# A norm applied on the transposed side: 1/std as a row through HBM, the mean folded into the weights

## The chip, the cores and the metric

The kernel runs on one core of a Trainium2 chip. The time is the device time in microseconds of that core, from the first to the last instruction. Engines are named as in the profile: PE (TensorE matmuls), PEld (its weight loads), DVE (VectorE), ACT (ScalarE), POOL (GpSimd), SP (SyncE, which here only issues transfers).

## The reference, cut to what matters

The input is (4, 128, 128, 128) in fp32: four images of 128 channels and 128 x 128 pixels. Layer 0 is a block that works on each pixel (token) by itself; layer 1 is a 3 x 3 convolution with a squeeze gate.

```python
def _block(x, ...):                       # every token t has 128 channels c
    t = x.reshape(b, c, h * w).transpose(0, 2, 1)
    t = _ln(t, ln0_g, ln0_b)
    y1 = _ln(t, ln1_g, ln1_b)
    att = jnp.einsum('btc,oc->bto', jax.nn.sigmoid(y1) * y1, W_out)
    t = t + att
    y2 = _ln(t, ln2_g, ln2_b)             # the norm that the change is about
    wht = jnp.einsum('btc,oc->bto', y2, W_whiten)
    k = jnp.square(jax.nn.relu(jnp.einsum('btc,hc->bth', wht, W_key)))      # 512 hidden
    kv = jnp.einsum('bth,ch->btc', k, W_value)
    r = jax.nn.sigmoid(jnp.einsum('btc,oc->bto', wht, W_recep))
    t = t + r * kv
    return t.transpose(0, 2, 1).reshape(b, c, h, w)
# _ln: (x - mean) * rsqrt(var + 1e-5) * g + b, over the 128 channels of a token
# ... layer 0: x = x + block(gn(x)) + the same block on the image turned; as the block works
#     on single tokens, both give the same, and the kernel computes it once
# ... layer 1: x = x + conv3x3(gn(x)) * gate
```

## The kernel before

Layer 0 handles a *group* of two chunks (h = 0, 1) of 512 pixels each. A group g passes through the operations of the list ORDER. One pass of the list is a *slot*: in slot s an entry `op:k` is issued for group s - k. Each engine runs its instructions in the order in which they are issued, so the list fixes the order on every engine. There are 64 groups; 20 slots after an image's first group its convolution begins, in the same slots.

```python
ORDER = """
    u1:0 Tu1:0 Tz21:3 u0:0 e1:1 bn01:0 Tu0:0 re02:3 tt0:2 bn00:0 c0:1 cp1:3 sq01:3 c2:1 S0:2
    q2:1 a:1 re00:3 y0:1 Tz11:1 pk10:3 z10:1 silu1:1 pk13:3 nb0:0 Tz10:1 re10:3 c5:1 re13:3
    y3:1 sq00:3 att1:1 pr0:3 p2:1 silu0:1 nb2:2 sq03:3 v0b:1 kv00:3 kv01:3 sq02:3 in1:0 b:1
    t1:0 att0:1 g1:0 v3:1 v4:1 v5a:0 th0:3 kv02:3 t0:0 in0:0 z20:2 b1:0 g0:0 pk12:3 pr1:3
    re12:3 bn11:0 T1:1 c3:1 sq12:3 T0:1 kv03:3 q0:3 pk11:3 e3:1 th1:3 sq13:3 v5b:0 Tz20:2
    b0:0 cp0:2 bn10:0 tt1:2 c4:0 re11:3 bn21:1 sq10:3 c:0 y2:0 kv10:3 x10:3 d:0 sq11:3 y1:0
    z21:2 pk03:2 S1:2 kv11:3 ca:0 q:0 pk01:2 p:0 kv12:3 bx0:3 kv13:3 nb1:0 v1:0 q1:3 x11:3
    bn20:1 c1:0 bx1:3 z11:0 re01:2 re03:2 pk00:2 v2:0 pk02:2 v0a:0 d8:0
"""

SQUARES = ("PAAA", "PAAA")

ON_GPSIMD = set()
ODD = {"v5a", "v5b", "c4", "c", "d", "y1", "y2", "ca", "d8", "c0", "y0", "c5", "y3"}
EVEN = {
    "p", "q", "v1", "v2", "p2", "q2", "c1", "e1", "c2", "a", "b", "v3", "v4", "c3", "e3",
```

The operations with their engines: `u` group norm of the input (ACT), `Tu` its transpose (PE), `bn` statistics per token (DVE), `nb` the terms of a norm (POOL), `t` norm 0 applied (ACT), `g`, `b` gain and shift (POOL), `z1`, `z2` norm 1 and norm 2 applied (ACT), `Tz` transposes of z (PE), `silu` (ACT), `att` (PE), `T` adds it to t (DVE), `cp` the input of the hidden layer brought from PSUM (ACT), `pk`, `pr`, `kv` the large matmuls (PE), `re`, `th` ReLU and tanh (ACT), `sq` the square (ACT or POOL, by SQUARES), `tt` the transpose of t for the residual (PE), `S`, `q` (DVE), `x` (POOL), `bx` and `in` statistics of the images (DVE). The names without a digit pair (`p`, `v1`, `c1`, `y0` and so on) are the convolution: `c` is PE, `e` ACT, the rest DVE.

Norm 0 and norm 1 and norm 2 are all applied with tokens on the partitions, where mean and 1/std of a token are scalars of a partition; the matmuls need channels on the partitions, so each z is transposed afterwards. PSUM banks come by tag; `tr` has two, used in turn.

```python
    def turned(src, tag, name):
        pt = bank(tag, name).rearrange("p (s c) -> p s c", s=SUB)
        for s in range(SUB):
            nc.tensor.transpose(pt[:, s, :], src[:, s, :], ident)
        return pt

    def scaled(dst, src, norm, h):
        rs, nb = norm
        for s in range(SUB):
            i = h * SUB + s
            nc.scalar.activation(
                dst[:, s, :], src[:, s, :], AF.Identity,
                bias=nb[:, i : i + 1], scale=rs[:, i : i + 1],
            )
    # ...
    def norm_terms(k, g):
        # ...
        gp, rs, nb, sm = nc.gpsimd, term("rs"), term("nb"), term("sm")
        gp.tensor_tensor(rs, st[:, :, 1], st[:, :, 4], ALU.subtract)
        gp.tensor_tensor(rs, rs, rs, ALU.mult)
        gp.tensor_scalar(rs, rs, C / 4, C * LN_EPS, ALU.mult, ALU.add)
        gp.tensor_tensor(sm, st[:, :, 2], st[:, :, 5], ALU.add)
        gp.tensor_tensor(rs, rs, sm, ALU.add)
        gp.tensor_tensor(rs, rs, nhalf, ALU.pow)
        gp.tensor_tensor(sm, st[:, :, 1], st[:, :, 4], ALU.add)
        gp.tensor_tensor(sm, sm, nhalf, ALU.mult)
        gp.tensor_tensor(nb, sm, rs, ALU.mult)
        S["norm", k, g] = rs, nb
    # ...
    def norm(k, g, h):
        S[f"z{k}", g, h] = z = sub_tile("z", "z", 3)
        scaled(z, S["t", g][:, h], S["norm", k, g], h)

    def norm_turned(k, g, h):
        S[f"z{k}t", g, h] = turned(S.pop((f"z{k}", g, h)), "tr", f"z{k}t")
    # ...
    def key_input(g, h):
        S["y2", g, h] = y = wk.tile([P, CH], F32, tag="y2", name="y2")
        nc.scalar.copy(y, flat(S.pop(("z2t", g, h))))

    def key(g, h, j):
        S["pk", g, h, j] = pk = bank("h", "pk")
        nc.tensor.matmul(pk, wk_s[:, ts(j, P)], S["y2", g, h], start=True, stop=True)
    # ...
    def t_turned(g, h):
        S["tt", g, h] = turned(S["t", g][:, h], "tr", "tt")

    def add_t(g, h):
        xs = chunk_of(g, h)
        nc.vector.scalar_tensor_tensor(
            xs, flat(S.pop(("tt", g, h))), 2.0, xs, ALU.mult, ALU.add
        )
```

The weights of the hidden layer are made once: the whitening matrix times the key and receptance matrices, with the gain of norm 2.

```python
    for src, n, dst, bias in ((wkt, HID, wk_s, kbias), (wrt, P, wr_s, rbias)):
        pw = bank("h", "pw")
        nc.tensor.matmul(pw[:, :n], ww, src, start=True, stop=True)
        raw = staged("raw", n)
        nc.vector.tensor_copy(raw, pw[:, :n])
        nc.vector.tensor_scalar(dst, raw, g2, None, ALU.mult)
        # ... the biases
```

Of the kernel before, what the change touches and what calls it, by code (L numbers as in the profile page):

```python
# [9 lines left out]
F32 = mybir.dt.float32  # L10
AF = mybir.ActivationFunctionType
ALU = mybir.AluOpType

P = 128
CH = 512
SUB = CH // P
# [6 lines left out]


ORDER = """
    u1:0 Tu1:0 Tz21:3 u0:0 e1:1 bn01:0 Tu0:0 re02:3 tt0:2 bn00:0 c0:1 cp1:3 sq01:3 c2:1 S0:2
    q2:1 a:1 re00:3 y0:1 Tz11:1 pk10:3 z10:1 silu1:1 pk13:3 nb0:0 Tz10:1 re10:3 c5:1 re13:3
    y3:1 sq00:3 att1:1 pr0:3 p2:1 silu0:1 nb2:2 sq03:3 v0b:1 kv00:3 kv01:3 sq02:3 in1:0 b:1
    t1:0 att0:1 g1:0 v3:1 v4:1 v5a:0 th0:3 kv02:3 t0:0 in0:0 z20:2 b1:0 g0:0 pk12:3 pr1:3
    re12:3 bn11:0 T1:1 c3:1 sq12:3 T0:1 kv03:3 q0:3 pk11:3 e3:1 th1:3 sq13:3 v5b:0 Tz20:2  # L30
    b0:0 cp0:2 bn10:0 tt1:2 c4:0 re11:3 bn21:1 sq10:3 c:0 y2:0 kv10:3 x10:3 d:0 sq11:3 y1:0
    z21:2 pk03:2 S1:2 kv11:3 ca:0 q:0 pk01:2 p:0 kv12:3 bx0:3 kv13:3 nb1:0 v1:0 q1:3 x11:3
    bn20:1 c1:0 bx1:3 z11:0 re01:2 re03:2 pk00:2 v2:0 pk02:2 v0a:0 d8:0
"""

SQUARES = ("PAAA", "PAAA")

ON_GPSIMD = set()
ODD = {"v5a", "v5b", "c4", "c", "d", "y1", "y2", "ca", "d8", "c0", "y0", "c5", "y3"}
# [7 lines left out]
def conv_preact_kernel(  # L47
# [40 lines left out]
    nc = tc.nc  # L88
    B, C, H, W = x.shape
    HID = w_key_t.shape[1]  # L90
# [7 lines left out]
    N = PAIR * SUB  # L98
# [3 lines left out]
    const = ctx.enter_context(tc.tile_pool(name="const", bufs=1))  # L102
# [2 lines left out]
    wk = ctx.enter_context(tc.tile_pool(name="wk", bufs=2))  # L105
    small = ctx.enter_context(tc.tile_pool(name="small", bufs=4))
    stat = ctx.enter_context(tc.tile_pool(name="stat", bufs=2))
    ps = ctx.enter_context(tc.tile_pool(name="ps", bufs=2, space=bass.MemoryType.PSUM))

    def bank(tag, name, bufs=2):  # L110
        return ps.tile([P, CH], F32, tag=tag, name=name, bufs=bufs)
# [30 lines left out]

    nhalf = const.tile([P, N], F32, tag="nhalf", name="nhalf")
    nc.gpsimd.memset(nhalf, -0.5)
    ones = const.tile([P, P], F32, tag="ones", name="ones")
    nc.gpsimd.memset(ones, 1.0)

    def load_const(name, src, shape):
        t = const.tile(shape, F32, tag=name, name=name)
# [22 lines left out]

    wk_s = const.tile([P, HID], F32, tag="wk_s", name="wk_s")
    wr_s = const.tile([P, P], F32, tag="wr_s", name="wr_s")
    kbias = const.tile([P, NH], F32, tag="kbias", name="kbias")
# [2 lines left out]
    def staged(name, n):  # L180
        return wk.tile([P, n], F32, tag="h", name=name, bufs=6)
# [5 lines left out]
    for src, n, dst, bias in ((wkt, HID, wk_s, kbias), (wrt, P, wr_s, rbias)):  # L187
        pw = bank("h", "pw")
        nc.tensor.matmul(pw[:, :n], ww, src, start=True, stop=True)
        raw = staged("raw", n)  # L190
        nc.vector.tensor_copy(raw, pw[:, :n])
        nc.vector.tensor_scalar(dst, raw, g2, None, ALU.mult)
        pb = bank("h", "pb")
        for j in range(n // P):
            nc.tensor.matmul(pb[:, j : j + 1], raw[:, ts(j, P)], b2, start=True, stop=True)
        nc.vector.tensor_copy(bias, pb[:, : n // P])
# [37 lines left out]
    def conv_setup(b):  # L234

        cw = wg.tile([P, 9, P], F32, tag="ring", name="cw", bufs=1)
        nc.sync.dma_start(cw, conv_w)
        d, mg, rs = yield from group_norm(st1.pop(b), "1")  # L240
        avg = col("avg")
        nc.vector.tensor_tensor(avg, d, rs, ALU.mult)
        mg6 = col("mg6")
        nc.vector.tensor_scalar(mg6, mg, 6.0, None, ALU.mult)
        yield
        p1 = bank("h", "p1")
        nc.tensor.matmul(p1[:NSE, 0:1], s1, avg, start=True, stop=True)
        yield
        a1 = stat.tile([NSE, 1], F32, tag="a1", name="a1")
        nc.vector.tensor_scalar(a1, p1[:NSE, 0:1], 0.0, None, ALU.max)  # L250
        yield
        p2 = bank("h", "p2")
        nc.tensor.matmul(p2[:, 0:1], s2, a1, start=True, stop=True)
        yield
        se = col("se")
        nc.scalar.activation(se, p2[:, 0:1], AF.Tanh, scale=0.5)
        yield
        nc.vector.tensor_scalar(se, se, 1.0, 0.5, ALU.add, ALU.mult)
        beta = col("beta")
        nc.vector.scalar_tensor_tensor(beta, se, cb, mg, ALU.mult, ALU.add)  # L260
        dg = wk.tile([P, P], F32, tag="u", name="dg")
        nc.vector.tensor_scalar(dg, ident, se, None, ALU.mult)
        yield
        pg = bank("h", "pg")
        nc.tensor.matmul(pg[:, :P], ones, dg, start=True, stop=True)
        yield
        row = wk.tile([P, P], F32, tag="u", name="row")
        nc.scalar.copy(row, pg[:, :P])
        yield
        nc.vector.scalar_tensor_tensor(  # L270
            cw, cw, rs, row.rearrange("p (o c) -> p o c", o=1).to_broadcast([P, 9, P]),
            ALU.mult, ALU.mult,
        )
        nc.vector.tensor_tensor(cw[:, 4], cw[:, 4], ident, ALU.add)
        yield
        w0, w1, w2 = (cw[:, 3 * a : 3 * a + 3].rearrange("p b c -> p (b c)") for a in range(3))
# [12 lines left out]
        yield
        for i in (1, 2):  # L290
            yield from form(i, None)
        nc.vector.scalar_tensor_tensor(u[1], tmp, -1.0 / 6, w6, ALU.mult, ALU.subtract)
        nc.vector.scalar_tensor_tensor(u[2], tmp, -1.0 / 6, w6, ALU.mult, ALU.add)
        yield
        w4 = wk.tile([P, 3 * P], F32, tag="z", name="w4", bufs=3)
        nc.scalar.mul(w4, w0, 0.25)
        nc.scalar.mul(w6, w6, 0.5)
        nc.vector.tensor_tensor(tmp, w4, w2, ALU.add)
        yield
        yield from form(3, None)  # L300
        yield from form(4, 1)
        nc.vector.scalar_tensor_tensor(u[3], tmp, 1.0 / 6, w6, ALU.mult, ALU.add)
        nc.vector.scalar_tensor_tensor(u[4], tmp, 1.0 / 6, w6, ALU.mult, ALU.subtract)
        yield
        yield from form(0, 2)
        nc.scalar.copy(u[0], w4)
        yield
        yield from form(5, 3)
        nc.scalar.copy(u[5], w2)
        gn1[b] = mg, mg6, beta  # L310
        uws[b] = uw

# [28 lines left out]
    def sub_tile(tag, name, bufs):  # L341
        return wk.tile([P, SUB, C], F32, tag=tag, name=name, bufs=bufs)
# [19 lines left out]
    def norm_terms(k, g):  # L362

        st = S.pop(("st", k, g))

        def term(name):
            return small.tile([P, N], F32, tag=f"{name}{k}", name=name, bufs=2)
# [5 lines that stand above are left out]
        gp.tensor_tensor(sm, st[:, :, 2], st[:, :, 5], ALU.add)  # L375
        gp.tensor_tensor(rs, rs, sm, ALU.add)
        gp.tensor_tensor(rs, rs, nhalf, ALU.pow)  # L377
        gp.tensor_tensor(sm, st[:, :, 1], st[:, :, 4], ALU.add)
        gp.tensor_tensor(sm, sm, nhalf, ALU.mult)
        gp.tensor_tensor(nb, sm, rs, ALU.mult)  # L380
        S["norm", k, g] = rs, nb

    def first_norm(g, h):
        if ("t", g) not in S:
# [9 lines left out]
        nc.gpsimd.tensor_tensor(t, t, over(b0), ALU.add)  # L394

    def norm(k, g, h):
        S[f"z{k}", g, h] = z = sub_tile("z", "z", 3)
        scaled(z, S["t", g][:, h], S["norm", k, g], h)

    def norm_turned(k, g, h):  # L400
# [12 lines left out]
    def attended(g, h):  # L413
        t = flat(S["t", g][:, h])
        nc.vector.tensor_tensor(t, S.pop(("att", g, h)), t, ALU.add)

    def key_input(g, h):
        S["y2", g, h] = y = wk.tile([P, CH], F32, tag="y2", name="y2")
        nc.scalar.copy(y, flat(S.pop(("z2t", g, h))))

    def key(g, h, j):
        S["pk", g, h, j] = pk = bank("h", "pk")
# [34 lines left out]
    def add_t(g, h):  # L457
        xs = chunk_of(g, h)
        nc.vector.scalar_tensor_tensor(
            xs, flat(S.pop(("tt", g, h))), 2.0, xs, ALU.mult, ALU.add  # L460
        )

    def gated(g, h):
# [140 lines left out]
    def layer0_op(op, g):  # L604
# [12 lines left out]
            "silu": lambda: silu(g, *d),  # L617
            "att": lambda: attend(g, *d),
            "T": lambda: attended(g, *d),
            "cp": lambda: key_input(g, *d),  # L620
            "pk": lambda: key(g, *d),
            "re": lambda: key_relu(g, *d),
# [121 lines left out]
```

## Time and profile before

The median of three runs is 2077.15 us (2076.03 to 2078.73). The profiled span is 2075.5 us.

| Engine | busy, us | share of the span |
|---|---|---|
| PE | 1896.8 | 91% |
| ACT | 1490.8 | 72% |
| POOL | 1324.9 | 64% |
| DVE | 1230.1 | 59% |
| PEld | 994.5 | 48% |

In the lines of the profile `out<-in` are the kernel's own names of the tiles, `xcount` the number of instructions, and a bracket or an arrow names the instruction that the engine waited for just before. L336 is `scaled` (norm 0, 1 and 2), L329 all transposes, L372 to L380 `norm_terms`, L390 and L394 gain and shift, L415 `attended`, L419 `key_input`, L423 `key`, L434 the squares on POOL, L449 `value`, L469 `add_gated`, L487 to L489 the convolution's matmuls. A matmul in fp32 stands as two instructions, a transpose as one.

### The profile page before, as it was taken

The numbers are of one execution on the slowest core, as the hardware profiler recorded it, in microseconds if no ns is written. First come the engines' busy times: TensorE is split into PE (matmuls) and PEld (weight loads), VectorE is DVE, ScalarE is ACT, GpSimd is POOL, SyncE is SP. The second block draws the span as 40 slices with busy tenths as digits, with TensorE's granted clock in tenths as the row PEclk, the third lists the DMA queues.
The fourth block names the chain that finished last, engine by engine and source line by source line (L and its number), as shares of the span: only waits on it lengthen the run. The fifth ranks groups of instructions, "written<-read, shape, count | busy, mean of one in ns | idle before, by whom it ended". The sixth has DMA issues, their size and how long they took to land.

```text
span 2075.5 us, 22706 instructions
## 1 busy us (share of the span) xinstructions
PE 1896.8 (91%) x6598; PEld 994.5 (48%) x6598; DVE 1230.1 (59%) x3082; ACT 1490.8 (72%) x3038; POOL 1324.9 (64%) x2259
## 2 busy tenths in 40 slices
PE   1388888888899999999999999999999999999898
PEld 1244444444455555555455555555455555554343
DVE  5334444434566666666766666665765566554897
ACT  1488888888777887778787887788788887874100
POOL 1667777777677776777677777777677777753000
PEclk9799999999999999999999999999999999999899
DMA  5100101001102211111012211110011111000011
GB/s 199 31 21 21 31 21 41 11 31 42 41 11 72 72 62 61 51 51 52 21 62 71 72 55 68 41 41 30 23 41 41 41 41 41 21 21 32 41 61 81
DMA packets 19116, 96.96 MB, mean 47 GB/s; under 512 B 2848, under 2 KB 4016, under 8 KB 10800
## 3 DMA queue, kind: packets, MB, share of 16 engines
q1 hardware_dynamic: 16704, 94.64, 12.7%
q10 hardware_dynamic: 2288, 0.87, 0.2%
q8 instruction: 52, 0.85, 0.2%
q14 instruction: 72, 0.59, 0.1%
HBM read 61.95 MB, written 33.55 MB: 46 GB/s over the span
## 4 chain that ended last, share of the span: by engine, by line
PE 34%; POOL 12%; ACT 2%; issue 1%; DVE 1%; POOLq 0%; DVEq 0%; ACTq 0%
PE pk L423 8%; PE kv L449 6%; PE m L487 5%; PE m L489 5%; PE m L488 5%; POOL rs L377 2%; POOL t L394 2%; POOL t L390 2%; PE pr L440 1%; POOL x L469 1%; POOL h L434 1%; PE att L411 1%; ACT z L336 1%; PE ut L329 1%; PE z1t L329 1%
## 5 line engine op out<-in xcount | busy, mean ns | idle before, releaser
L336 ACT ACTIVATE z<-t,nb,rs 128x128 f32<-128x128 f32 x1024 | 421.1, 487 | 187.4 <-POOL nb L380 187.1
L423 PE MATMUL pk<-y,wk_s 128*128 128x512 f32 x1024 | 514.9, 605 | 36.1 <-ACT h L427 34.4
L449 PE MATMUL kv<-h,wv 128*128 128x512 f32 x1024 | 513.1, 604 | 28.2 <-POOL h L434 19.3
L360 DVE BATCH_NORM_STATS2 st<-t 128x6 f32<-128x128 f32 x1024 | 216.3, 278 | 366.9 <-POOL t L394 366.9
L427 ACT ACTIVATE h<-pk,kbias 128x512 f32<-128x512 f32 x512 | 341.1, 682 | 52.2 <-PE pk L423 45.2
L377 POOL TENSOR_TENSOR rs<-rs,nhalf 128x8 f32<-128x8 f32 x192 | 318.2, 1657 | 15.0
L423 PEld LDWEIGHTS pk<-y,wk_s 128*128 128x128 f32 x1024 | 185.4, 191 | 273.1 <-issue 144.4
L449 PEld LDWEIGHTS kv<-h,wv 128*128 128x128 f32 x1024 | 185.0, 192 | 240.2 <-issue 167.8
L469 POOL TENSOR_TENSOR x<-x,r 128x512 f32<-128x512 f32 x128 | 176.2, 1376 | 162.3 <-DVE r L465 154.4
L432 ACT ACTIVATE h<-h 128x512 f32<-128x512 f32 x384 | 234.6, 629 | 4.0
L372 POOL TENSOR_TENSOR rs<-st 128x8 f32<-128x8 f32 x192 | 53.5, 279 | 266.1 <-DVE st L360 266.1
L336 ACT ACTIVATE t<-ut,nb,rs 128x128 f32<-128x128 f32 x512 | 193.9, 479 | 9.2 <-POOL nb L380 9.2
L487 PE MATMUL m<-v,uw 128*128 128x512 f32 x384 | 197.9, 598 | 0.7 <-ACT e L559 0.7
L488 PE MATMUL m<-v,uw 128*128 128x508 f32 x384 | 196.6, 594 | 0.0
L489 PE MATMUL m<-v,uw 128*128 128x508 f32 x384 | 196.3, 593 | 0.0
L465 DVE SCALAR_TENSOR_TENSOR r<-r,kv 128x512 f32<-128x512 f32 x128 | 87.8, 686 | 160.0 <-PE kv L449 139.3
L394 POOL TENSOR_TENSOR t<-t,b 128x512 f32<-128x512 f32 x128 | 163.1, 1274 | 10.1
L390 POOL TENSOR_TENSOR t<-t,g 128x512 f32<-128x512 f32 x128 | 162.9, 1273 | 3.2 <-ACT t L336 3.2
L411 PEld LDWEIGHTS att<-wo,y 128*128 128x128 f32 x1024 | 131.4, 192 | 49.9 <-issue 26.4
L411 PE MATMUL att<-wo,y 128*128 128x128 f32 x1024 | 137.2, 277 | 6.4 <-ACT y L405 6.4
L360 DVE BATCH_NORM_STATS2 st<-ut 128x6 f32<-128x128 f32 x512 | 109.9, 283 | 52.7 <-PE ut L329 52.7
L434 POOL TENSOR_TENSOR h<-h 128x512 f32<-128x512 f32 x128 | 133.4, 1042 | 10.1 <-ACT h L427 10.1
(121 smaller groups left out, 2646.1 us busy)
## 6 DMA issues: line engine op xcount, KB each, us to landing
x<-in_x SPq DMA_DIRECT2D x32, 1024.0 KB, 4.9
out<-x SPq DMA_DIRECT2D x32, 1024.0 KB, 3.9
xs<-in_x SPq DMA_DIRECT2D x48, 512.0 KB, 3.7
cw<-in_conv_w SPq DMA_DIRECT2D x4, 576.0 KB, 5.8
wv<-in_w_value_t ACTq DMA_DIRECT2D x1, 256.0 KB, 6.6
wkt<-in_w_key_t ACTq DMA_DIRECT2D x1, 256.0 KB, 7.5
g<-in_ln_g ACTq DMA_DIRECT2D x1, 64.0 KB, 4.3
b<-in_ln_b ACTq DMA_DIRECT2D x1, 64.0 KB, 5.8
```

The lines of the kernel that those rows point to most:

```text
L336: nc.scalar.activation(dst[:, s, :], src[:, s, :], AF.Identity, bias=nb[:, i : i + 1], scale=rs[:, i : i + 1],)
L360: nc.vector.bn_stats(st[:, h * SUB + s, :], src[:, s, :])
L377: gp.tensor_tensor(rs, rs, nhalf, ALU.pow)
L394: nc.gpsimd.tensor_tensor(t, t, over(b0), ALU.add)
L411: nc.tensor.matmul(att[:, ts(s, P)], y[:, ts(s, P)], wo, start=True, stop=True)
L423: nc.tensor.matmul(pk, wk_s[:, ts(j, P)], S["y2", g, h], start=True, stop=True)
L427: nc.scalar.activation(k, S["pk", g, h, j], AF.Relu, bias=kbias[:, j : j + 1])
L432: nc.scalar.activation(k, k, AF.Square)
L449: nc.tensor.matmul(S["kv", g, h], wv[:, j, :], S.pop(("h", g, h, j)), start=(j == 0), stop=(j == NH - 1))
L487: nc.tensor.matmul(pc, u[:, 1], v, start=True, stop=False)
L488: nc.tensor.matmul(pc[:, :, 1:W], u[:, 0], v[:, :, 0 : W - 1], start=False, stop=False)
L489: nc.tensor.matmul(pc[:, :, 0 : W - 1], u[:, 2], v[:, :, 1:W], start=False, stop=True)
```

## The change

Norm 2 is no longer applied with tokens on the partitions. Its mean goes into the weights: the matmul sums over channels, so subtracting from each column of the weights its mean over the channels has the same effect as subtracting the mean of the token. What is left of the norm is the factor 1/std of each token. On the side where channels are on the partitions this is a row, the same for all partitions. It is made so: the 128 x 8 block of 1/std of a group is transposed on PE (`Tr`), copied out of PSUM (`rc`), written to a small HBM buffer (`W`), and read back spread over all 128 partitions, once for each chunk (`R0`, `R1`). `cp` is now a multiply on DVE of the transpose of t, which the residual needs anyway (`tt`), with that row. The activations `z2`, the transposes `Tz2` and the copy on ACT go away.

With it come a new ORDER, all squares on ACT, two buffers for z instead of three, and a matrix of 1/128 where there was one of ones.

```diff
# ...
 
 
 ORDER = """
-    u1:0 Tu1:0 Tz21:3 u0:0 e1:1 bn01:0 Tu0:0 re02:3 tt0:2 bn00:0 c0:1 cp1:3 sq01:3 c2:1 S0:2
-    q2:1 a:1 re00:3 y0:1 Tz11:1 pk10:3 z10:1 silu1:1 pk13:3 nb0:0 Tz10:1 re10:3 c5:1 re13:3
-    y3:1 sq00:3 att1:1 pr0:3 p2:1 silu0:1 nb2:2 sq03:3 v0b:1 kv00:3 kv01:3 sq02:3 in1:0 b:1
-    t1:0 att0:1 g1:0 v3:1 v4:1 v5a:0 th0:3 kv02:3 t0:0 in0:0 z20:2 b1:0 g0:0 pk12:3 pr1:3
-    re12:3 bn11:0 T1:1 c3:1 sq12:3 T0:1 kv03:3 q0:3 pk11:3 e3:1 th1:3 sq13:3 v5b:0 Tz20:2
-    b0:0 cp0:2 bn10:0 tt1:2 c4:0 re11:3 bn21:1 sq10:3 c:0 y2:0 kv10:3 x10:3 d:0 sq11:3 y1:0
-    z21:2 pk03:2 S1:2 kv11:3 ca:0 q:0 pk01:2 p:0 kv12:3 bx0:3 kv13:3 nb1:0 v1:0 q1:3 x11:3
-    bn20:1 c1:0 bx1:3 z11:0 re01:2 re03:2 pk00:2 v2:0 pk02:2 v0a:0 d8:0
+    u1:0 Tu1:0 u0:0 x11:3 Tz10:1 Tu0:0 bn01:0 bn00:0 z11:1 bx1:3 v1:1 pr0:2 Tz11:1 q2:1
+    silu0:1 p2:1 re00:2 sq00:2 y2:1 ca:1 att0:1 silu1:1 c0:1 pk01:2 nb0:0 d8:1 kv00:2 T0:1
+    y0:1 th0:2 t1:0 bn20:1 v3:1 tt1:2 g1:0 re01:2 in0:0 c1:1 cp1:2 e1:1 att1:1 pk02:2 c3:1
+    T1:1 bn21:1 pk10:2 c5:1 b1:0 y3:1 re02:2 S1:2 t0:0 nb2:1 e3:1 pk03:2 v2:1 g0:0 b0:0
+    re10:2 c2:1 in1:0 a:1 pk12:2 sq01:2 sq10:2 Tr:1 v0a:1 sq02:2 re03:2 sq03:2 re12:2 b:1
+    kv01:2 kv02:2 rc:1 pk13:2 re13:2 v4:1 pk11:2 kv03:2 sq12:2 c4:0 bn11:0 v5a:0 tt0:1
+    bn10:0 v0b:1 pr1:2 q0:2 c:0 d:0 re11:2 sq11:2 S0:1 sq13:2 kv10:2 v5b:0 kv11:2 th1:2
+    kv12:2 kv13:2 nb1:0 W:1 y1:0 R0:1 z10:0 q:0 cp0:1 pk00:1 R1:1 x10:2 p:0 bx0:2 q1:2
 """
 
-SQUARES = ("PAAA", "PAAA")
+SQUARES = ("AAAA", "AAAA")
 
 ON_GPSIMD = set()
 ODD = {"v5a", "v5b", "c4", "c", "d", "y1", "y2", "ca", "d8", "c0", "y0", "c5", "y3"}
# ...
     wk = ctx.enter_context(tc.tile_pool(name="wk", bufs=2))
     small = ctx.enter_context(tc.tile_pool(name="small", bufs=4))
     stat = ctx.enter_context(tc.tile_pool(name="stat", bufs=2))
+    dram = ctx.enter_context(tc.tile_pool(name="dram", bufs=2, space=bass.MemoryType.DRAM))
     ps = ctx.enter_context(tc.tile_pool(name="ps", bufs=2, space=bass.MemoryType.PSUM))
 
     def bank(tag, name, bufs=2):
# ...
 
     nhalf = const.tile([P, N], F32, tag="nhalf", name="nhalf")
     nc.gpsimd.memset(nhalf, -0.5)
-    ones = const.tile([P, P], F32, tag="ones", name="ones")
-    nc.gpsimd.memset(ones, 1.0)
+    mean_of = const.tile([P, P], F32, tag="mean_of", name="mean_of")
+    nc.gpsimd.memset(mean_of, 1.0 / C)
 
     def load_const(name, src, shape):
         t = const.tile(shape, F32, tag=name, name=name)
# ...
     for src, n, dst, bias in ((wkt, HID, wk_s, kbias), (wrt, P, wr_s, rbias)):
         pw = bank("h", "pw")
         nc.tensor.matmul(pw[:, :n], ww, src, start=True, stop=True)
-        raw = staged("raw", n)
+        raw, raw2 = staged("raw", n), staged("raw2", HID)
         nc.vector.tensor_copy(raw, pw[:, :n])
-        nc.vector.tensor_scalar(dst, raw, g2, None, ALU.mult)
+        nc.vector.tensor_scalar(raw2[:, :n], raw, g2, None, ALU.mult)
+        pc = bank("h", "pc")
+        nc.tensor.matmul(pc[:, :n], mean_of, raw2[:, :n], start=True, stop=True)
+        nc.vector.tensor_tensor(dst, raw2[:, :n], pc[:, :n], ALU.subtract)
         pb = bank("h", "pb")
         for j in range(n // P):
             nc.tensor.matmul(pb[:, j : j + 1], raw[:, ts(j, P)], b2, start=True, stop=True)
# ...
         gp.tensor_tensor(sm, st[:, :, 2], st[:, :, 5], ALU.add)
         gp.tensor_tensor(rs, rs, sm, ALU.add)
         gp.tensor_tensor(rs, rs, nhalf, ALU.pow)
+        S["norm", k, g] = rs, nb
+        if k == 2:
+            return
         gp.tensor_tensor(sm, st[:, :, 1], st[:, :, 4], ALU.add)
         gp.tensor_tensor(sm, sm, nhalf, ALU.mult)
         gp.tensor_tensor(nb, sm, rs, ALU.mult)
-        S["norm", k, g] = rs, nb
 
     def first_norm(g, h):
         if ("t", g) not in S:
# ...
         nc.gpsimd.tensor_tensor(t, t, over(b0), ALU.add)
 
     def norm(k, g, h):
-        S[f"z{k}", g, h] = z = sub_tile("z", "z", 3)
+        S[f"z{k}", g, h] = z = sub_tile("z", "z", 2)
         scaled(z, S["t", g][:, h], S["norm", k, g], h)
 
     def norm_turned(k, g, h):
# ...
         t = flat(S["t", g][:, h])
         nc.vector.tensor_tensor(t, S.pop(("att", g, h)), t, ALU.add)
 
+
+
+    def turn_std(g):
+        rs, _ = S.pop(("norm", 2, g))
+        S["rt", g] = rt = bank("tr", "rt")
+        nc.tensor.transpose(rt[:N, :P], rs, ident)
+
+    def copy_std(g):
+        S["rrow", g] = row = small.tile([N, P], F32, tag="rrow", name="rrow", bufs=1)
+        nc.vector.tensor_copy(row, S.pop(("rt", g))[:N, :P])
+
+    def store_std(g):
+        S["rd", g] = rd = dram.tile([N, P], F32, tag="rd", name="rd")
+        nc.sync.dma_start(rd, S.pop(("rrow", g)))
+
+    def spread_std(g, h):
+        S["R", g, h] = r = wk.tile([P, CH], F32, tag="R", name="R", bufs=3)
+        src = S["rd", g][h * SUB : (h + 1) * SUB, :]
+        nc.sync.dma_start(r, src.rearrange("(o s) c -> o (s c)", o=1).to_broadcast([P, CH]))
+
     def key_input(g, h):
         S["y2", g, h] = y = wk.tile([P, CH], F32, tag="y2", name="y2")
-        nc.scalar.copy(y, flat(S.pop(("z2t", g, h))))
+        nc.vector.tensor_tensor(y, flat(S["tt", g, h]), S.pop(("R", g, h)), ALU.mult)
 
     def key(g, h, j):
         S["pk", g, h, j] = pk = bank("h", "pk")
# ...
     def add_t(g, h):
         xs = chunk_of(g, h)
         nc.vector.scalar_tensor_tensor(
-            xs, flat(S.pop(("tt", g, h))), 2.0, xs, ALU.mult, ALU.add
+            xs, flat(S["tt", g, h]), 2.0, xs, ALU.mult, ALU.add
         )
 
     def gated(g, h):
# ...
             "silu": lambda: silu(g, *d),
             "att": lambda: attend(g, *d),
             "T": lambda: attended(g, *d),
+            "Tr": lambda: turn_std(g),
+            "rc": lambda: copy_std(g),
+            "W": lambda: store_std(g),
+            "R": lambda: spread_std(g, *d),
             "cp": lambda: key_input(g, *d),
             "pk": lambda: key(g, *d),
             "re": lambda: key_relu(g, *d),
# ... the matrix of ones in the gate's setup becomes mean_of, with a factor C on its result;
# ... two scratch tiles of the convolution's setup on tag "z" go to bufs=2
```

## The prediction

> **What bounds the kernel now.** I read the engine table, then stretches of the run, then single slots. A slot is one pass of the ORDER list: all 64 groups (two chunks of 512 pixels each) enter in turn, one per slot.
>
> ```profile
> PE 1896.8 (91%) x6598; PEld 994.5 (48%) x6598; DVE 1230.1 (59%) x3082; ACT 1490.8 (72%) x3038; POOL 1324.9 (64%) x2259
> ```
>
> PE is far ahead, but 91% over the whole run hides two regimes. I took the slot borders from the starts of the two u activations (L347), which stand once in each slot, and asked for the busy time between them:
>
> ```profile
> 133.02:527.84 394.82, 338.72 (x1265) 177.22 (x1264) 169.60 (x515) 333.13 (x692) 287.73 (x526) 0.99 0.09 27
> 588.30:1813.46 1225.16, 1210.00 (x4315) 643.39 (x4314) 787.38 (x1974) 977.96 (x1990) 890.40 (x1475) 1.00 0.14 48
> ```
>
> The columns are length, busy PE, PEld, DVE, ACT, POOL, the granted clock, DMA share and GB/s. Up to 528 us the convolution has not begun: 15 slots of 394.82/15 = 26.3 us, in which no engine is full (PE 86%, ACT 84%, POOL 73%). From 588 us there are 42 slots of 1225.16/42 = 29.2 us with PE at 98.8%. Here only PE work counts.
>
> The early regime is explained by one slot. The POOL rows, each with start, length and operation:
>
> ```profile
> 268.24 0.21 POOL L372 TENSOR_TENSOR rs<-st 128x8 f32<-128x8 f32 x1 [3.99 <-DVE st L360]
> ...
> 271.98 1.04 POOL L434 TENSOR_TENSOR h<-h 128x512 f32<-128x512 f32 x1
> 272.98 0.21 POOL L372 TENSOR_TENSOR rs<-st 128x8 f32<-128x8 f32 x1
> ...
> 276.70 1.27 POOL L390 TENSOR_TENSOR t<-t,g 128x512 f32<-128x512 f32 x1
> 278.06 1.26 POOL L394 TENSOR_TENSOR t<-t,b 128x512 f32<-128x512 f32 x1
> 279.29 1.27 POOL L390 TENSOR_TENSOR t<-t,g 128x512 f32<-128x512 f32 x1
> 280.63 1.27 POOL L394 TENSOR_TENSOR t<-t,b 128x512 f32<-128x512 f32 x1
> 281.87 1.03 POOL L434 TENSOR_TENSOR h<-h 128x512 f32<-128x512 f32 x1
> 282.87 1.27 POOL L469 TENSOR_TENSOR x<-x,r 128x512 f32<-128x512 f32 x1
> ```
>
> and what ACT does when the last of this is done:
>
> ```profile
> 287.93 1.65 ACT L336 ACTIVATE z<-t,nb,rs 128x128 f32<-128x128 f32 x4 [2.99 <-POOL nb L380]
> 289.48 1.24 ACT L427 ACTIVATE h<-pk,kbias 128x512 f32<-128x512 f32 x2
> 290.62 1.51 ACT L347 ACTIVATE u<-x,nb,rs 128x512 f32<-128x512 f32 x2
> ```
>
> This is a loop: u (264.36), its transposes and statistics (POOL starts at 268.24), then POOL without a gap to 287.9 (nb of norm 0, a square, nb of norm 2, gain and shift twice, a square, an add, nb of norm 1), then z1 and two ReLUs on ACT, then the next u at 290.62: 26.26 us, the slot. So early on POOL's chain is the bound; ACT waits 2.99 us for it.
>
> For the PE regime I need what an operation costs in the stream, not its listed length:
>
> ```profile
> 909.80 0.60 PE L329 MATMUL ut<-ident,u 128*128 128x128 f32 x4
> 910.24 0.60 PE L329 MATMUL z2t<-ident,z 128*128 128x128 f32 x4
> 910.67 0.60 PE L329 MATMUL ut<-ident,u 128*128 128x128 f32 x4
> 911.11 0.60 PE L329 MATMUL tt<-ident,t 128*128 128x128 f32 x4
> 911.55 1.02 PE L487 MATMUL m<-v,uw 128*128 128x512 f32 x2
> 912.41 1.01 PE L488 MATMUL m<-v,uw 128*128 128x508 f32 x2
> ```
>
> From start to start, four transposes take 0.437 us and a 512-column matmul (two instructions) 0.857 us. A slot holds 32 transposes (3.50), 8 att (in the same timeline 0.89 per four, 1.78), 8 pk, 8 kv and 2 pr (18 x 0.857 = 15.43) and, on average, 9 conv matmuls (7.70): 28.4 us, close to the 28.7 us from one plain slot to the next. The sum is complete.
>
> **What the Trainium skill says.** "Trainium Kernel Development and Optimization", section Performance Expectations, calls matmul busy time a bad metric because matmuls are pipelined; the trace agrees (277 ns listed for a transpose, 109 ns apart), so I count starts. "VectorE: DVE Perf Modes", section The TRN2 errata, gives (N+151)/0.96 ns for an fp32 tensor_tensor, 691 ns at 512; the trace has 677 ns for L415, PSUM plus SBUF, the very form of the new multiply. "DMA: Bandwidth & Descriptors", section Anatomy of one DMA, puts some 2.0 us of fixed cost plus bytes/436e3 us on a transfer of the GpSimd path, most of it the wait until the write is confirmed. In this trace, on the SP queue, 512 KB took 3.7 us and 1024 KB to HBM 3.9 us: the same size.
>
> **The change, part by part.**
>
> *PE.* Removed per group: the eight transposes of z2, 8 x 0.109 = 0.87 us. Added: one transpose of the 128x8 block of 1/std, 0.1 us by estimate (no more than one transpose). Net -0.77 us. t was transposed already, for the residual; key_input now reads the same PSUM bank.
>
> *ACT.* Removed: eight z2 activations (1.65 per four, 0.41 apart: 3.3 us) and two copies (584 ns: 1.2). Added: the two squares from POOL (629 ns: 1.3). Net -3.2 us of about 22.2.
>
> *POOL.* Removed: two squares (1.04 each) and the last three operations of norm 2's terms (217, 250 and 226 ns): 2.8 us per slot.
>
> *DVE.* Added: two multiplies (0.68) and a copy of 8x128 (0.2): 1.6 us on 18.7 (787.38/42): 20 of 28 us. Not a bound.
>
> *DMA.* Added per group on SP: 4 KB out to HBM, then two spreads of 256 KB back. Bandwidth is nothing (DMA share 0.14); latency is the question. By the estimate from the skill's formula, W takes 2.0 and R 2.0 + 0.6 us, 4.6 together; I take 5 to 6. In the new order W follows rc, and cp0 must be ready when PE reaches pk00, its last operation of the slot. Between Tr and pk00 PE has kv01, kv02, pk13, pk11, kv03, tt0, pr1 and kv10 to kv13: 10 x 0.857 + 0.44 = 9.0 us, in odd slots c4 too (2.6). The chain Tr 0.3, rc 0.3, W and R0 5.5, cp0 0.7, semaphores 0.4 is 7.2 us. It fits with 1.8 us to spare.
>
> *The early loop, new order.* On POOL now nb0, g1, b1, nb2, g0, b0, nb1, x10; on ACT z10 closes the slot. From u: 3.9 us to nb0's start, nb0 3.75, t1 on ACT 1.6 (no longer hidden behind a square), g1 and b1 2.6, nb2 without its three operations 3.05, g0 and b0 2.55, the last statistics on DVE 0.95, nb1 3.75, z10 1.65, then u: 23.8 us. PE's in-order list adds some tenths, as pk00 runs just before the next slot's first transposes. I take 24.2: 2.1 us saved in each of 15 slots, 31 us.
>
> *The full regime.* 42 slots x 0.77 = 32 us, and 2 more in the two slots around it that are also full. The new list's loop (23.8 us plus DVE's convolution work ahead of bn10) ends under 27.7 us even in the slots with the even conv list, where bn10 stands behind rc: by my count u is ready 0.6 us before PE wants it.
>
> *Lag.* pk, kv and pr come two slots after u instead of three. When the convolution starts, most of one group's hidden layer is done already, inside the early slots where PE has room. That is up to 8 pk and 8 kv, 13.7 us, out of the full stretch; I count 10.
>
> *Preamble.* Folding the mean needs two more matmuls and two DVE passes ahead of the statistics of the first image: +2 us.
>
> Sum: 31 + 34 + 10 - 2 = 73 us. For waits that a hand count misses (a bank shared by rt and tt, W behind a 1 MB store on the same queue) I give back 6: 67 us, 2077 - 67 = 2010 us.
>
> **Rivals.**
>
> *The round trip through HBM is late.* If W and R together took 10 us instead of 5.5, pk00 would wait some 2.7 us in slots without c4, i.e. in each early slot and every second full one: 15 x 2.7 + 21 x 2.7 = 97 us, all of the gain and more, about 2090 us. For it: three dependent transfers on one in-order queue, with stores of 1 MB between, and 128 reads of the same 2 KB. Against it: 256 KB is small, and transfers of two and four times the size land in 3.7 to 3.9 us. This is the main way to lose; one chance in ten for a large part of it.
>
> *The early slots give nothing.* PE reaches Tr early and waits for nb2, then has 9 us left in its list. If PE idles there for long and the granted clock falls, as at 68 to 94 us (0.62 in that stretch), the early slots stay near 26 us. Then 2035 to 2040 us. One in six.
>
> *PE's saving is not realised in the full regime.* DVE, now with the multiply on the path to pk, delays PE, and slots stay near 29 us. Against it: DVE is at 64% there. Then 2040 us. One in eight.
>
> *Better than counted.* If the lighter ACT and POOL also remove the remaining 1.2% of PE idleness: 15 us more, 1990 us.
>
> **Range and chances.** Both main terms right: 1985 to 2015 us. One failing: 2035 to 2045 us. The round trip failing: over 2050 us. So 1983 to 2046 us for eight in ten. Faster by over 2% means under 2035.6 us: all but the cases in which one whole term fails: 0.85. Within 2%: 0.11. Slower: 0.04.
>
> **What would show it.** z2t gone and the slots after 600 us about 28.4 us apart with PE still near 99% busy: the PE step is right. u starts 24 us apart before 530 us: the early loop is right. No or little wait of pk on DVE's y (the multiply), nor of DVE's y on a DMA: the round trip is hidden; R landing within 3.5 us and W within 2.5 us. I am wrong if pk waits for y by more than a few tenths of a us per slot, if Tr's wait on POOL appears in the full regime, or if the slots grow though PE's work shrank.

## The result, and the profile after

The changed kernel takes 2001.97 us (median; 1998.43 to 2006.08). Its ratio to the kernel before, which took 2077.94 us beside it, is 0.9636, with a 95% interval of 0.9616 to 0.9656: 3.6% less. The prediction was 2010 us.

The profiled span is 1999.4 us. First the engine table of the kernel after:

```profile
PE 1835.4 (92%) x6154; PEld 937.8 (47%) x6154; DVE 1338.9 (67%) x3276; ACT 1297.7 (65%) x2526; POOL 1151.2 (58%) x1939
```

PE lost 61 us of busy time, ACT 193, POOL 174; DVE gained 109. The span lost 76. None of these changes in busy time is the change of the span, so the run has to be cut into stretches. These are the stretches of the kernel after that answer to the two shown of before, from slot 4 to slot 19 and from slot 21 to slot 63 (length, busy PE, PEld, DVE, ACT, POOL, granted clock, DMA share, GB/s):

```profile
137.46:495.19 357.73, 315.69 (x1160) 164.33 (x1160) 196.17 (x560) 289.67 (x571) 249.79 (x451) 0.99 0.16 52
547.52:1743.52 1196.00, 1179.87 (x4020) 607.66 (x4019) 857.91 (x2100) 849.98 (x1654) 777.58 (x1264) 1.00 0.19 69
```

An early slot is now 357.73/15 = 23.85 us (26.3 before), a full one 1196.00/42 = 28.48 us (29.17), with PE still at 98.7%. The starts of the u activations give the whole account:

| Stretch | before, us | after, us | gained | predicted |
|---|---|---|---|---|
| up to the first u | 39.49 | 43.99 | -4.5 | -2 |
| slots 0 to 3 | 93.53 | 93.47 | 0.1 | 0 |
| slots 4 to 18, no convolution | 394.82 | 357.73 | 37.1 | 31 |
| slots 19 and 20 | 60.46 | 52.33 | 8.1 | with the last row |
| slots 21 to 62, full | 1225.16 | 1196.00 | 29.2 | 32 |
| from slot 63 to the end | 262.04 | 255.88 | 6.2 | 12 with slots 19 and 20 |

The rows differ in how well they repeat. The two long stretches do: in e3 and e7 below, which leave these parts alone or nearly so, the slots are again 23.85 and 23.87 us early, and 28.47 and 28.48 us full. The first and the last row do not: the last part took 255.2 to 259.2 us in e3, e6, e7 and e8, and the first u of kernels with the same preamble came between 42.4 and 44.0 us.

In the lines that follow, L341 is `scaled`, L352 the u, L365 the statistics per token, L377 to L388 `norm_terms`, L397 and L401 gain and shift, L437 the store of the row of 1/std, L442 its spread, L446 the multiply, L450 `key`, L454 the ReLU. Edits in the experiments move some of these numbers by a few.

Next the POOL rows of one early slot (start, length, operation, the wait before it), which stand against those of before:

```profile
284.43 0.21 POOL L377 TENSOR_TENSOR rs<-st 128x8 f32<-128x8 f32 x1 [1.02 <-DVE st L365]
...
289.82 1.28 POOL L397 TENSOR_TENSOR t<-t,g 128x512 f32<-128x512 f32 x1 [1.61 <-ACT t L341]
291.17 1.27 POOL L401 TENSOR_TENSOR t<-t,b 128x512 f32<-128x512 f32 x1
292.40 0.21 POOL L377 TENSOR_TENSOR rs<-st 128x8 f32<-128x8 f32 x1
...
299.01 0.21 POOL L377 TENSOR_TENSOR rs<-st 128x8 f32<-128x8 f32 x1 [0.99 <-DVE st L365]
```

and the end of the loop on ACT:

```profile
302.81 1.65 ACT L341 ACTIVATE z<-t,nb,rs 128x128 f32<-128x128 f32 x4 [0.73 <-POOL nb L388]
304.36 1.51 ACT L352 ACTIVATE u<-x,nb,rs 128x512 f32<-128x512 f32 x2
```

This is the loop that the prediction added up: terms of norm 0, a wait for t (1.61), gain and shift, terms of norm 2 without their last three operations, gain and shift, a wait for the statistics (0.99), terms of norm 1, z, u. The slot began with u at 280.82; 23.54 us, against 23.8 counted. Between the stages POOL has small waits now, but the same loop still ends last. The wait that the second rival of the prediction named is there too: in the early slots PE waited 20.3 us in all, 15 times, for the 1/std that it transposes. It did not make the slots longer than the loop, and the granted clock stayed at 0.99.

The round trip through HBM, on SP's queue, in an early slot:

```profile
296.11 0.28 SPq L437 DMA_DIRECT2D rd<-rrow  x1
297.37 0.80 SPq L442 DMA_DIRECT2D R<-rd  x2
```

and in a full slot in which a block of the output is stored just before:

```profile
650.16 0.34 SPq L611 DMA_DIRECT2D out<-x  x1
651.52 0.28 SPq L437 DMA_DIRECT2D rd<-rrow  x1
654.17 0.80 SPq L442 DMA_DIRECT2D R<-rd  x2
```

R is issued when the row has landed in HBM: 1.26 us after the row's own issue in the first case, 2.65 us with a store of 1 MB ahead. In the second case the multiply started at 657.69 us, after a wait for R, 3.5 us after the issue of R. Two of the prediction's own signs for a hidden trip, 2.5 us for W and 3.5 us for R, were thus passed or reached in such a slot. What the run waits for in all because of it (engine, line, releaser, total us, times, longest):

```profile
DVE y L446 <- DMA R<-rd: 10.2, 13, 2.1
...
PE pk L450 <- DVE y L446: 6.5, 3, 4.8
```

Of 128 multiplies 13 waited for their row, and three times PE waited for the multiply. Whether these waits cost time is asked by an experiment below.

### The profile page after: what moved, and what is told of

It is laid out like the page before. It is cut to its first block, busy times and chain, and to the rows that moved or that the text cites. A ratio compares the mean times of both kernels' runs of the same rounds, so it can differ in the third digit from the quotient of the medians.

```text
span 1999.4 us, 21672 instructions
## 1 busy us (share of the span) xinstructions
PE 1835.4 (92%) x6154; PEld 937.8 (47%) x6154; DVE 1338.9 (67%) x3276; ACT 1297.7 (65%) x2526; POOL 1151.2 (58%) x1939
## 4 chain that ended last, share of the span: by engine, by line
PE 69%; POOL 12%; DVE 7%; ACT 6%; issue 3%; DMA 2%; ACTq 0%; POOLq 0%; DVEq 0%
PE kv L476 18%; PE pk L450 15%; PE m L514 8%; PE m L515 7%; PE m L516 7%; POOL rs L382 5%; PE pr L467 4%; PE att L418 3%; DVE st L365 3%; ACT t L341 2%; PE ut L334 2%; PE tt L334 2%; PE z1t L334 2%; POOL t L401 1%; ACT z L341 1%
## 5 line engine op out<-in xcount | busy, mean ns | idle before, releaser
L450 PE MATMUL pk<-y,wk_s 128*128 128x512 f32 x1024 | 507.6, 601 | 32.1 <-ACT h L454 23.6
L476 PE MATMUL kv<-h,wv 128*128 128x512 f32 x1024 | 484.8, 596 | 1.4 <-DVE r L492 1.4
L454 ACT ACTIVATE h<-pk,kbias 128x512 f32<-128x512 f32 x512 | 350.8, 689 | 174.5 <-PE pk L450 173.1
L459 ACT ACTIVATE h<-h 128x512 f32<-128x512 f32 x512 | 302.4, 635 | 6.1
L476 PEld LDWEIGHTS kv<-h,wv 128*128 128x128 f32 x1024 | 190.3, 191 | 231.6 <-issue 195.2
L450 PEld LDWEIGHTS pk<-y,wk_s 128*128 128x128 f32 x1024 | 181.2, 190 | 246.1 <-issue 135.9
L341 ACT ACTIVATE t<-ut,nb,rs 128x128 f32<-128x128 f32 x512 | 192.6, 465 | 157.0 <-POOL nb L388 157.0
L496 POOL TENSOR_TENSOR x<-x,r 128x512 f32<-128x512 f32 x128 | 163.1, 1275 | 172.1 <-DVE r L492 172.1
L365 DVE BATCH_NORM_STATS2 st<-t 128x6 f32<-128x128 f32 x1024 | 221.3, 276 | 51.0 <-POOL t L401 47.5
L341 ACT ACTIVATE z<-t,nb,rs 128x128 f32<-128x128 f32 x512 | 209.7, 481 | 52.4 <-POOL nb L388 52.4
L397 POOL TENSOR_TENSOR t<-t,g 128x512 f32<-128x512 f32 x128 | 163.6, 1278 | 101.4 <-ACT t L341 101.4
L377 POOL TENSOR_TENSOR rs<-st 128x8 f32<-128x8 f32 x192 | 56.9, 297 | 258.3 <-DVE st L365 247.2
L401 POOL TENSOR_TENSOR t<-t,b 128x512 f32<-128x512 f32 x128 | 163.5, 1277 | 10.0
L467 PE MATMUL pr<-y,wr_s 128*128 128x512 f32 x256 | 132.0, 597 | 8.0 <-ACT h L454 8.0
L365 DVE BATCH_NORM_STATS2 st<-ut 128x6 f32<-128x128 f32 x512 | 111.0, 282 | 37.5 <-PE ut L334 37.5
L418 PEld LDWEIGHTS att<-wo,y 128*128 128x128 f32 x1024 | 126.0, 192 | 13.9 <-issue 6.6
```

Source lines behind the costliest of these rows:

```text
L341: nc.scalar.activation(dst[:, s, :], src[:, s, :], AF.Identity, bias=nb[:, i : i + 1], scale=rs[:, i : i + 1],)
L365: nc.vector.bn_stats(st[:, h * SUB + s, :], src[:, s, :])
L418: nc.tensor.matmul(att[:, ts(s, P)], y[:, ts(s, P)], wo, start=True, stop=True)
L454: nc.scalar.activation(k, S["pk", g, h, j], AF.Relu, bias=kbias[:, j : j + 1])
L459: nc.scalar.activation(k, k, AF.Square)
L467: nc.tensor.matmul(pr, wr_s, S["y2", g, h], start=True, stop=True)
```

## The experiments

All but e5 change the kernel after, so their times stand against 2002 us; e5 changes the kernel before. The kernel before was run again beside each of them and its median moved between 2075.1 and 2077.9 us, so a difference of some 3 us to 2002 says nothing by itself; the lengths of the slots say more. e1 to e12 name the runs.

### Eight transposes put back (e1)

```diff
-        S["tt", g, h] = turned(S["t", g][:, h], "tr", "tt")
+        S["tt", g, h] = pt = turned(S["t", g][:, h], "tr", "tt")
+        for s in range(SUB):
+            nc.tensor.transpose(pt[:, s, :], S["t", g][:, h, s], ident)
```

> The changed kernel with t transposed twice into the same bank: the eight PE transposes that the change saved are put back, as work without use; all else as in the changed kernel (2002 us). Theory (PE's queue bounds the slots with convolution, the early slots are bound by a chain through POOL): the full slots grow by 8 x 0.109 = 0.87 us from 28.5 to 29.3 us, the early slots stay within 0.3 us of 24; 44 x 0.87 = 38 us, 2040 us. Rival (the full slots became shorter through the lighter ACT and POOL or through the new order, not through PE work): less than 10 us, under 2012 us.

Measured: 2033.18 us, ratio to before 0.9799 (0.9784 to 0.9813); 31 us more. Early slots 24.2 us, full slots 29.00. The stretch of full slots:

```profile
553.71:1771.65 1217.94, 1206.93 (x4354) 646.57 (x4353) 851.59 (x2099) 851.28 (x1654) 781.48 (x1265) 1.00 0.19 67
```

The rival's "less than 10 us" is out: PE work without any use costs time in the full slots. But 0.87 us more work made the slot only 0.52 us longer; PE went from 98.7% to 99.1%. Two plain full slots of the kernel after, a long and a short one, last 56.0 us, and hold 55.3 us of PE work by the prediction's count. By this estimate the work put back fills the 0.7 us in which PE had nothing to do and adds the rest, 2 x 0.87 - 0.7 = 1.0 us; such a pair of e1 lasts 57.1 us, 1.1 more. One thing PE's work does not explain: e1 gives PE one transpose more per slot than the kernel before had, and its full slots are still 0.17 us shorter than the 29.17 of before. So a small part of the gain in the full slots comes from something else, the new order for instance; no run shows what it is.

### Squares: both, the first, the second on POOL (e2, e9, e10)

```diff
-SQUARES = ("AAAA", "AAAA")
+SQUARES = ("PAAA", "PAAA")   # e2;  e9: ("PAAA", "AAAA");  e10: ("AAAA", "PAAA")
```

> The changed kernel with one square per chunk back on POOL (1.04 us each). Theory (early slots are POOL's chain): only the second of the two stands inside the chain of the new list, the first falls into the time in which POOL waits for the statistics of u; early slots 24 to 25 us, full slots unchanged; 16 x 1.0 = +16 us, about 2018 us. Rival (ACT is the limit of the early slots, and a square taken from it pays): early slots shorter, about 1990 us. Rival 2 (the place of the squares is of no account): within 5 us of 2002 us.

Measured: 2085.55 us, ratio 1.005 (1.0033 to 1.0067): the whole gain is gone. Early slots 25.6 us, full slots 29.68. All three expectations missed. The loop did grow, but by 1.75 us in an early slot and 1.2 in a full one, which had been expected to stay. The two halves tell the squares apart.

> The changed kernel with only the first of the two squares back on POOL, ahead of the terms of norm 0 in POOL's queue. After e2 (83 us more, where 16 were expected) the theory is: this square waits for its ReLU on ACT, and the terms of norm 0, ready some 0.7 us earlier, wait behind it in POOL's queue; they start 1.75 us later, and with them t, and on ACT all that stands behind t, the copy that frees the convolution's bank among it. So this one square makes nearly all of it: early slots 25.4 to 25.7 us, full slots 29.4 to 29.7, 2070 to 2086 us. Rival (the two squares cost alike, by POOL's time): half, about 2043 us.

> The changed kernel with only the second square back on POOL, between shift and the terms of norm 1. Theory as in e9: there POOL waits 0.99 us for the statistics anyway, so the square costs next to nothing: early slots under 24.2 us, full slots under 28.6, 2000 to 2010 us. Rival (the two squares cost alike): about 2043 us.

Measured: the first alone 2076.71 us, ratio 1.000 (0.9991 to 1.0008), early slots 25.6, full 29.49, all in the ranges expected. The second alone 2011.21 us, ratio 0.9681 (0.9665 to 0.9697), early 23.9, full 28.66, 1 us above its expected range. The 64 squares of a run (1.04 us each, 67 us together) cost 75 us in the first place and 9 us in the second: 1.75 and 0.05 us per early slot, 1.0 and 0.2 us per full slot. POOL's rows of an early slot with the first:

```profile
272.20 1.04 POOL L461 TENSOR_TENSOR h<-h 128x512 f32<-128x512 f32 x1 [1.05 <-ACT h L454]
273.20 0.21 POOL L377 TENSOR_TENSOR rs<-st 128x8 f32<-128x8 f32 x1
```

POOL waits 1.05 us for the ReLU, then squares, and only then come the terms of norm 0, whose statistics DVE had finished at 272.1 us, 1.1 us earlier. With them waits t on ACT, for 3.15 us instead of 1.23, and behind t in ACT's queue, in a full slot, the operation (L584) that frees the single bank of the convolution. PE then stands, as in this row of e2:

```profile
650.68 1.13 PE L514 MATMUL m<-v,uw 128*128 128x512 f32 x2 [1.33 <-ACT e L584]
```

Over the full slots of e9 these waits sum to 25.9 us, against 4.9 in the kernel after. So the full slots are close to a second bound: the edit that lengthened the early slot, which the loop sets, by 1.75 us, lengthened the full one by 1.0 us. If the same delay is what both feel, it has some 0.7 us to spare in a full slot; this is an inference from the two growths, since PE waits there for the convolution's bank and not for u.

### No round trip (e3)

```diff
-        nc.sync.dma_start(rd, S.pop(("rrow", g)))
+        S.pop(("rrow", g))
...
-        S["R", g, h] = r = wk.tile([P, CH], F32, tag="R", name="R", bufs=3)
-        nc.sync.dma_start(r, src.rearrange("(o s) c -> o (s c)", o=1).to_broadcast([P, CH]))
+        S["R", g, h] = one_row        # a constant row of ones
```

> The changed kernel without the store to HBM and the two spreads: the multiply takes a constant row of ones. It leaves out the factor 1/std of norm 2. The transpose of 1/std and its copy out of PSUM stay. Theory (the round trip is hidden but for some slots, whose waits on R sum to 10 us on DVE in the profile): 0 to 8 us less, 1994 to 2002 us, early slots unchanged. Rival (the trip or its traffic is a hidden bound): early or full slots shorter by 1 us and more, below 1960 us.

Measured: 2002.09 us, ratio 0.9651 (0.9637 to 0.9665); early 23.85, full 28.47 us. Without store, spreads and the 34 MB that they read, the time is the same: the trip is hidden whole, and the few waits for it in the profile after cost nothing that can be measured.

### The trip twice (e4)

```diff
+        first = dram.tile([N, P], F32, tag="rd1", name="rd1")
+        nc.sync.dma_start(first, row)
+        nc.sync.dma_start(row, first)
         S["rd", g] = rd = dram.tile([N, P], F32, tag="rd", name="rd")
         nc.sync.dma_start(rd, row)
```

> The changed kernel with the row of 1/std written to HBM, read back to SBUF, and written a second time before it is spread: some 3 us more before R (the store's issue to R's issue takes 1.26 us in the profile, the read back by estimate 1.5 to 2). Theory (hidden with 2 to 4 us to spare, least in slots in which an image block is stored just before): the early slots stay within 0.5 us, every second full slot grows by 1 to 2 us; 10 to 40 us more, 2012 to 2042 us. Rival (the trip stands on the path): 3 us in each of 64 slots, about 2190 us. Rival 2 (much to spare): within 5 us of 2002 us.

Measured: 2038.66 us, ratio 0.9824 (0.9809 to 0.9838); 37 us more. Early slots 24.0 (+0.15), full slots 29.22 (+0.74); of these, every second one grew, by 0.5 to 3.6 us, the others by nothing to speak of. SP's rows in an early slot:

```profile
296.28 0.29 SPq L438 DMA_DIRECT2D rd<-rrow  x1
297.50 0.28 SPq L439 DMA_DIRECT2D rrow<-rd  x1
298.80 0.26 SPq L441 DMA_DIRECT2D rd<-rrow  x1
300.00 0.82 SPq L446 DMA_DIRECT2D R<-rd  x2
```

and the waits:

```profile
DVE y L450 <- DMA R<-rd: 103.4, 41, 4.1
...
PE pk L454 <- DVE y L450: 30.3, 27, 7.6
```

R is issued 3.72 us after the first row instead of 1.26, 2.5 us later. That is absorbed in the early slots and in the full slots without a store, and shows after every store: in the slot with the store at 655.16 us, R is issued 5.28 us after the first row instead of 2.65. The spare time is about 2.5 us or more where nothing is stored ahead. With a store it is, by estimate, about 1 us on average: 2.6 us more delay, and 2 x 0.74 = 1.5 us more time per two slots.

### Before, with its squares on ACT (e5)

```diff
-SQUARES = ("PAAA", "PAAA")
+SQUARES = ("AAAA", "AAAA")
```

> The kernel before with one edit: all squares on ACT, as in the changed kernel; norm 2, its transposes and the order as they were. It asks how much of the early gain comes from taking 2 x 1.04 us out of POOL's chain alone. Theory (the early slots are that chain): early slots from 26.3 to about 24.4 us, as ACT is at 84% and takes 1.3 us more; full slots unchanged at 28.7 to 29.2; 15 x 1.9 = 29 us, about 2048 us. Rival (ACT or PE bounds the early slots): no gain or a loss, 2077 us and more.

Measured: 2074.6 us, ratio 0.9984 (0.9978 to 0.9991). Early slots fell to 24.9 us, by 1.4 where the theory has 1.9; but the full slots rose from 29.17 to 29.59, and 15 x 1.4 = 21 us came and 42 x 0.42 = 18 us went. PE's largest wait, which in the kernel before is 8.8 us:

```profile
PE kv L449 <- ACT h L432: 60.6, 46, 3.3
```

In the old order the squares on ACT come late for kv. So more than half of the early gain (1.4 of 2.5 us per slot) is to be had without the new norm, but with this list the full slots take it back. Whether another list would keep it without the new norm, no run shows.

### Gain and shift on DVE in the early slots (e6); the weights moved (e7); both (e8)

```diff
-        nc.gpsimd.tensor_tensor(t, t, over(g0), ALU.mult)       # and the shift alike
+        eng = nc.vector if g < NP + LAG else nc.gpsimd
+        eng.tensor_tensor(t, t, over(g0), ALU.mult)             # e6; g1 behind bn21 in ORDER
```

> The changed kernel with gain and shift (four operations of 1.27 us on POOL) on DVE for the first 20 groups, which run before the convolution; in the list the first gain moves behind the statistics of the attended t. Theory (POOL's chain bounds the early slots, PE comes next with 19.9 us of work and its wait for the transposed 1/std): early slots 21.5 to 22.5 us; 16 x 1.9 = 30 us less, about 1972 us, full slots unchanged. Rival (ACT's or PE's order is the bound of the early slots already): early slots stay above 23.3 us, gain below 10 us.

Measured: 1986.9 us, ratio 0.9555 (0.9536 to 0.9575): 15 us less, half of what was expected. Early slots 22.95 us; slots 19 and 20 took 2.2 us more.

```diff
-    for src, n, dst, bias in ((wkt, HID, wk_s, kbias), (wrt, P, wr_s, rbias)):   # in the preamble
+    def weights():       # the same operations, with yields between them
...
+            if s == 0:
+                chains.append(weights())
```

> The changed kernel with the making of the hidden layer's weights (with the mean folded in) moved from the preamble into slot 0. Theory (the fold costs time because its DVE operations wait for PE while the statistics of the first image stand behind them in DVE's queue): the first u at 36 to 38 us instead of 44, the slots after it unchanged; 6 to 8 us less, about 1995 us. Rival (the arrival of the first image bounds the preamble): first u at 42 us or later, time within 2 us of 2002 us.

Measured: 1997.81 us, ratio 0.9608 (0.9593 to 0.9622). The first u starts at 38.55 us, just outside the 36 to 38 expected, but slot 0 takes 22.6 us instead of 20.8, and slot 4 starts at 135.64 us instead of 137.46. The 4 us less are not clear of noise: the two intervals meet.

> The two edits of e6 and e7 together. If both theories hold and the two are independent: 30 + 7 us less, about 1965 us.

Measured: 1981.66 us, ratio 0.9537 (0.9522 to 0.9551): 20 us less where e6 and e7 give 15 and 4. The sum fits, but the traces do not show that the two add as thought: e8 has its first u at 38.2 us and starts slot 4 at 131.1, e6 has 42.6 and 130.3. What the earlier u gains is gone by slot 4. Most of the distance to the expected 1965 us is the miss of e6.

### One ReLU ahead of t, everywhere (e11) and late only (e12)

```diff
-... th0:2 t1:0 bn20:1 v3:1 tt1:2 re01:2 ...
+... th0:2 re01:2 t1:0 bn20:1 v3:1 tt1:2 ...      # on top of e8; e12: only from slot 20 on
```

> The version of e8 with one ReLU (re01) moved ahead of t in ACT's queue. In e8 the early slots stand at 22.7 us with PE at 91%; ACT sits idle 2.04 us ahead of t, waiting for the terms of norm 0, while this ReLU's input is ready and PE waits 0.94 us for the bank that it frees. Theory (queue order on ACT, not load, holds PE back in both regimes): early slots about 21.8 us (16 x 0.9 = 14 us), full slots shorter by 0.1 to 0.2 us, since the copy that frees the convolution's bank also moves up (4 to 8 us): about 1962 us. Rival (something else ends last): within 4 us of e8's 1982 us.

Measured: 1994.89 us, ratio 0.9603 (0.9589 to 0.9617), 13 us worse than e8. The full slots did fall, 28.56 to 28.41; the early ones rose from 22.84 to 24.1. There the ReLU no longer held PE, but PE reached the transpose of 1/std sooner and waited for POOL (1.6 us in the slot at 276 us, where e8 has 0.5). Over the early slots PE's waits for the ReLU fell by 9 us and those for POOL rose by 15, which leaves most of the 19 us lost there open; so is why every second early slot grew by more than the other.

> The version of e8, with e11's place of the ReLU only from slot 20 on, when the convolution runs. In e11 the full slots fell from 28.56 to 28.41 us as expected, while the early slots rose from 22.8 to 24.1 us, since there the ReLU gained PE nothing: the transpose of 1/std waited for POOL either way. Theory (the two regimes have different last waits and take the two orders independently): early slots at 22.8 us, full slots at 28.4; 42 x 0.15 = 6 us under e8, about 1976 us. Rival (the change of order at slot 20 costs a bubble, or e8's 1982 us is the limit): within 2 us of 1982 us.

Measured: 1976.72 us, ratio 0.9509 (0.9496 to 0.9522); early 22.95, full 28.41 us. This is the fastest version here; its interval and that of e8 meet at their edges, and its full slots are shorter by the 0.15 us expected.

## Why the prediction held

*The early loop* was the largest term, 31 us, and gave 37.1. The loop itself was counted right (23.8, measured 23.5 to 24.4); I had added 0.4 us per slot for PE's order, which was not needed. Its parts agree too: from u to the terms of norm 0 3.6 us (3.9 counted), from there to the first gain 5.4 (5.35), on to the terms of norm 1 9.2 (9.15), and on to u 5.35 (5.4). That the chain through POOL was the bound is shown three times: e5 takes the squares out of it in the kernel before and the early slot falls by 1.4 us; e9 puts one square ahead of the terms of norm 0 and it grows by 1.75 us; e6 shortens the chain and it falls by 0.9 us, until something else ends last.

*The full regime* was predicted at 0.77 us per slot and gave 0.69. e1 says how much of it is PE's: with the transposes back 0.52 of the 0.69 are gone. The step is right, and its limit shows too: PE is the bound with some 0.35 us per slot unused by the estimate under e1, and a second bound stands, by the inference under e9, some 0.7 us behind it. The 0.6 us of my count is near that, but it was counted for u, and the waits of e9 are for the convolution's bank; the nearness may be chance.

*Lag* was put at 10 us, with 2 for the slots around; slots 19, 20 and the end gave 14.3, of which the end's part repeats only within some 4 us. The trace agrees with the mechanism, though no run isolates it: before slot 20 the kernel before had issued 276 pk, 270 kv and 68 pr instructions, the kernel after 290, 288 and 72. That is 36 more at 0.43 us, 15 us of PE work done while PE had room.

*The round trip* was counted to fit with 1.8 us to spare. e3 and e4 bracket it: nothing is gained without it, and some 2.5 us more is too much only in slots with a store. W was quicker than my 2.0 us (1.26), and slower behind a store (2.65), which I had named but not sized.

*The preamble* reads 4.5 us in the table, where 2 were said, but most of the excess is not the change. PE's first matmul waits for a weight to arrive, before and after:

```profile
16.27 2.04 PE L189 MATMUL pw<-wkt,ww 128*128 128x512 f32 x2 [16.27 <-DMA wkt<-in_w_key_t]
19.09 2.05 PE L191 MATMUL pw<-wkt,ww 128*128 128x512 f32 x2 [19.09 <-DMA wkt<-in_w_key_t]
```

From there to the first u it takes 23.2 us before (39.49) and 24.9 us after (43.99): the fold costs 1.7 us, near the 2 us counted. The other 2.8 us are the arrival of the weight, which differs from execution to execution whatever the preamble: e5, with the preamble of before, had it at 18.29 us and its first u at 41.50, again 23.2 us later; the seven runs with the preamble of after had it at 17.0 to 18.3 us and the first u 24.9 to 25.5 us later. e7 takes more out of the preamble than the fold, namely the whole making of the weights, so its first u (38.55 us) is earlier than that of the kernel before.

*The allowance* of 6 us for waits that a hand count misses was not used up; with it left out the prediction would have been 2004 us. That the sum of 73 us comes so near the 76 measured is in part luck: the early loop gave 6 us more than said and the lag 2 more, the full slots 3 less and the first row 2.5 less. No run separates the new list from the new norm, as the operations in the two lists differ; what each is worth alone is known only as far as e1 and e5 tell.

My count was weaker where it had not been written down step by step. The expectation for e2 rested on the same loop, but I put the first square into POOL's wait for u without asking when its own input comes.

## What to carry to other kernels

Cut a run where its bound changes before adding up a gain: here one change took 37 us from a loop through four engines and 29 us from a full PE, and the busy shares of the whole run would have named neither. In an in-order queue the place of an operation decides what it costs: a square of 1.04 us made the early slot 1.75 us longer in one place and 0.05 us in another, because what stands behind it waits for its inputs too. A trip through HBM was free here because the other queues held more work between its two ends than it takes; measure that distance by doubling the trip, not only by removing it. And before a small term of one pair of profiles is explained, look at the same stretch in the other runs: the preamble moved by 2 us between executions of the same instructions.

## What the runs showed of the hardware

Moving gain and shift to DVE in e6 and e8 made POOL's small operations slower while they ran. POOL's terms of norm 2 in an early slot of e8:

```profile
323.19 0.52 POOL L381 TENSOR_TENSOR rs<-st 128x8 f32<-128x8 f32 x1 [2.22 <-DVE st L369]
323.78 0.64 POOL L382 TENSOR_TENSOR rs<-rs 128x8 f32<-128x8 f32 x1
...
325.33 1.97 POOL L386 TENSOR_TENSOR rs<-rs,nhalf 128x8 f32<-128x8 f32 x1
```

The same three take 0.21, 0.20 and 1.64 us in the kernel after, and DVE runs its gains and shifts from 322.96 to 324.4 and from 325.09 to 326.5 us. The Trainium skill, "GPSIMD Engine Reference", section Specifications, says that POOL shares its way to SBUF with VectorE and contends with DVE instructions that have two SBUF inputs, as gain and shift have; the rows agree: the three take 1.1 us longer in this slot. PE then waited 0.53 us for them, so up to that much of what e6 fell short by may come from here; no run isolates it.
